# Convolution, attention and mixture of experts on one core: the last part in a fixed periodic order, transposes moved to VectorE, roots moved to ScalarE

## The chip, the core and the metric

The kernel runs on one core of a Trainium2 chip. The core has five engines that run side by side, each of them in the order in which its instructions were written: TensorE (PE in the profile; its weight loads are listed as PEld), VectorE (DVE), ScalarE (ACT), GpSimd (POOL) and SyncE (SP), which here only issues DMAs. An instruction waits on semaphores until what it needs is there, and everything behind it on its engine waits with it. The metric is the device time of one launch in microseconds; the median of several runs counts.

## The reference

Thirty-two images of 128 channels and 64 x 64 pixels go through three steps. Cut to what matters:

```python
# layer 0: butterfly transforms along h and w, one mix over channels per frequency, and back
x = x + conv(gn(x))                       # complex; real part is taken
# layer 1: 4096 tokens of 128 channels per image
t = tokens(x)
n = ln(t)                                 # mean and variance of each token, eps 1e-5
k, v = n @ Wk.T + bk, n @ Wv.T + bv
probs = softmax(einsum('sbe,sbf->sef', k, v) / sqrt(seq_len))
t = t + einsum('sef,sbf->sbe', probs, n)
n = ln(t)
p = softmax(n @ router_w + router_b)      # 8 experts, the best 2 with renewed weights
t = t + sum over the best 2 of p * (n @ expert_w[e] + expert_b[e])
x = channels(t)                           # back to (128, 64, 64)
```

For the attention, `seq_len` is the size of the first axis, 32, and each image has its own 128 x 128 table of scores. All arithmetic is in 32-bit floats.

## The kernel before

The kernel has three parts. The first transforms every image, the second mixes channels per frequency; the last products of the mixing start at 2527.08 us. The third part, which the change is about, takes everything after that: inverse transform, attention, experts, and the way back to channels. It handles image after image, and three images are in work at once: while image b is in its inverse transform (`conv`), b-1 is in its attention (`front`), and b-2 in its experts (`experts`).

**Names of the steps.** Each step is added to a planner under a short key; the profile shows tile names and lines.

- `r0..r7` (SP, L887) load the mixed frequencies of an image from DRAM, `x` (SP, L879) loads the image itself. `w0..w7` (PE, tile pu, L903) transform along w, `wo` (ACT, tile u, L913) copies out, `h0..h3` (PE, tile py, L925) transform along h, `ho` (DVE, L933) adds to the image tile y.
- `pt0..pt7` (PE, L1049) turn 512 pixels each from channels to tokens, four 128 x 128 transposes; `to` (ACT, L1054) copies into the token buffer tk (two buffers, one for even, one for odd images); `sa` (DVE, L1021) takes statistics. `va` (DVE, six small operations on 128 x 32 values, L1031 to L1036) makes variances of them, `pwa` (POOL, L1041) takes the power -0.5, `na` (DVE, L1078 and L1079) makes the shift.
- `xg` (ACT, L1089) normalizes, `pg` (PE, L1100) makes the Gram matrix, then a short chain of small steps (`gs`, `pb`, `t1`, `pb2`, `sm`, `pr`, `sr`, `sn`, `pc`, `prx`) makes the softmax. `pp` (PE, L1173) applies it to the image tile (the image is the stationary operand), `at` (ACT, L1186) scales, `ad` (DVE, L1201) adds to tk.
- `vb`, `pwb`, `nb` do the same as `va`, `pwa`, `na` for the second norm (`nb`: L1240 and L1241). `lg`, `l2`, `f1` to `f5`, `gt` (DVE, L1232 to L1276) make logits, find the best two experts and their gates.
- `xn` (ACT, L1301) normalizes, `px` (PE, L1311) transposes, `xT` (ACT, L1317) copies, `pe` (PE, L1324) multiplies 128 tokens by four experts, `m` (DVE, L1335) weighs the result out of PSUM, `s` (POOL, L1360 to L1363, five operations) sums over experts into tk.
- `st` (PE, tile po, L1370) transposes 512 tokens back to channels, and `so` (ACT, L1376) copies them to SBUF and issues one DMA of 256 KB to the output (L1377).

**What sets the order.** The planner (`Plan.run`) is a list scheduler that runs when the program is built: each step has an engine, an estimated cost, a due time (with offsets in `SHIFT`), the steps it follows, and the buffers it takes and frees. Buffers matter below: `pe` has three PSUM banks, shared by the expert products, so the fourth product waits until `m` has read the first; `tl` has three banks for all of `pt`, `px`, `st`, `pg`, `pp` and the softmax chain; `cv` is one tile for `w` and `h`.

Of the kernel before, what the change touches and what calls it, by code (L numbers as in the profile page):

```python
# [24 lines left out]
class Plan:  # L25
# [12 lines left out]
    def run(self):  # L38
# [46 lines left out]
        self.length = now  # L85
        for i in order:
            ops[i][3]()
# [3 lines left out]
def kernel(  # L91
# [737 lines left out]
    def prepare():  # L829
# [23 lines left out]
    plan = Plan({"cv": 1, "pe": 3, "tl": 3, "r": 10, "x": 2, "xg": NG, "xn": 2, "xT": 2, "tm": 2, "so": 2, "gate": 2})  # L853
    SLOT = 114.0

    SHIFT = {
        "ad": -0.15, "at": -0.25, "f": 0.71, "gs": -1.97, "gt": 0.71, "h": -0.24, "ho": -3.5, "kvp": 3.43,
        "kvq": -0.45, "l": 0.71, "lg": 3.61, "m": -0.32, "na": -1.87, "nb": -0.81, "pb": -1.97, "pc": -1.97,
        "pe": 0.16, "pg": -0.08, "pp": 0.19, "pr": -1.97, "prx": -1.97, "pt": -0.23, "pwa": -1.87, "pwb": 3.61,
        "px": 0.15, "r": -0.04, "s": 0.08, "sa": 1.29, "sm": -1.97, "sn": -1.97, "so": 2.13, "sr": -1.97,  # L860
        "st": 1.1, "t": -1.97, "to": 0.06, "va": -1.87, "vb": 3.61, "w": 0.28, "x": -0.68, "xT": -0.68,
        "xg": 0.21, "xn": 2.42,
    }
    made = {}

    def add(b, key, engine, us, at, run, after=(), take=(), free=(), late=0.0):


        names = [k if isinstance(k, tuple) else (b, k) for k in after]
        at += SHIFT.get(key.rstrip("0123456789_"), 0.0)  # L870
        made[b, key] = plan.add(
            engine, us, SLOT * at, run, [made[k] for k in names if k[0] >= 0], take, free, late
        )


    def transfers(b):
        def load_x():
            xs[b] = xp.tile([P, HW, HW], F32, tag="x", name=f"y{b}")
            nc.sync.dma_start(xs[b].rearrange("c h w -> c (h w)"), xv[b])  # L879

        def load_r(e):
            def run():
                i = 8 * b + e
                ring, tag = (rp, "r") if i % 10 < 8 else (rp2, "r2")
                t = rs[b, e] = ring.tile([P, 16 * n], F32, tag=tag, name=f"r{b}_{e}")
                for r in range(2):
                    nc.sync.dma_start(t[r * n : (r + 1) * n], pfv[b, e, r])  # L887
            return run

        for e in range(8):  # L890
            add(
                b, f"r{e}", "SP", 0.2, b - 0.5 + 0.08 * e, load_r(e) if b else (lambda: None), take=("r",),
                late=5.0 if b else 0.0,
            )
        add(b, "x", "SP", 0.1, b + 0.2, load_x if b else (lambda: None), take=("x",), late=12.0 if b else 0.0)

    def conv(b):
        def w_inverse(e):

            def run():  # L900
                ps = tile_of["cv", b, e] = cps.tile([P, 8, P], F32, tag="cv", name=f"pu{b}_{e}")
                for k in range(8):
                    nc.tensor.matmul(  # L903
                        ps[:, k, :], rs[b, e][:, k * P : (k + 1) * P], qw.rearrange("w r m -> w (r m)"),
                        start=True, stop=True,
                    )
            return run
# [31 lines left out]
        def w_inverse_piece(e, oh):  # L939

            def run():
                ps = tile_of["cw", b, e, oh] = eps.tile([P, 8, n], F32, tag="pe", name=f"pw{b}_{e}_{oh}")
                for k in range(8):
                    lo = (2 * k + oh) * n
                    for r in range(2):
                        nc.tensor.matmul(
                            ps[r * n : (r + 1) * n, k, :], rs[b, e][:, lo : lo + n], qw[:, r, :], start=True, stop=True
                        )
            return run
# [28 lines left out]
        if b < 2:  # L978
            for e in range(8):
                at = b + 0.08 * e  # L980
                for oh in range(2):
                    add(
                        b, f"w{e}_{oh}", "PE", 0.95, at + 0.04 * oh, w_inverse_piece(e, oh),
                        [f"r{e}"] + [(b - 1, f"h{k}") for k in range(4)], ("pe",), ("r",) if oh else (),
# [13 lines left out]
            if b == 0:  # L998
                add(b, "prep", "PE", 3.5, 0.98, prepare, ["h3"], ("pe",), ("pe",))
# [14 lines left out]
    def front(b):  # L1014
# [24 lines left out]
        def power(which):  # L1039
            total, var, nmr, rstd = v[which]  # L1040
            nc.gpsimd.tensor_tensor(rstd, var, mhalf, ALU.pow)  # L1041

        def turn(g):
            def run():
                ps = tile_of["pt", b, g] = tps.tile([P, 512], F32, tag="tl", name=f"pt{b}_{g}")
                x1 = xs[b].rearrange("c h w -> c (h w)")
                for k in range(4):
                    i = 4 * g + k
                    nc.tensor.transpose(ps[:, k * P : (k + 1) * P], x1[:, i * P : (i + 1) * P], ident)  # L1049
# [18 lines left out]
        for g in range(8):  # L1068
            at = s1 + 0.016 * g
            add(b, f"pt{g}", "PE", 0.48, at, turn(g), [(b - 2, f"st{g}")] + [f"ho{k}" for k in range(4)], ("tl",))  # L1070
            add(b, f"to{g}", "ACT", 0.55, at, turned(g), [f"pt{g}"], (), ("tl",))
            add(b, f"sa{g}", "DVE", 0.85, at, stats1(g), [f"to{g}"] + (["sa0"] if g else []))
        add(b, "va", "DVE", 1.7, s1 + 0.14, lambda: moments(1), [f"sa{g}" for g in range(8)])
        add(b, "pwa", "POOL", 5.5, s1 + 0.14, lambda: power(1), ["va"])

        def nmr1():
            total, var, nmr, rstd = v[1]
# [3 lines left out]
        add(b, "na", "DVE", 0.9, s1 + 0.14, nmr1, ["pwa"])  # L1081
# [74 lines left out]
        add(b, "pb", "PE", 0.35, at, kv1, ["gs"], ("tl",))  # L1156
# [10 lines left out]
        def product(lo, m):  # L1167
            def run():
                x1 = xs[b].rearrange("c h w -> c (h w)")
                ps = tile_of["pp", b, lo] = tps.tile([P, 512], F32, tag="tl", name=f"pp{b}_{lo}")  # L1170
                for k in range(m):
                    i = lo + k
                    nc.tensor.matmul(  # L1173
                        ps[:, k * QX : (k + 1) * QX], x1[:, i * P : (i + 1) * P], prx[b % 2], start=True, stop=True
# [30 lines left out]
        for j, lo in enumerate(range(0, NT, 3)):  # L1205
            m = min(3, NT - lo)
            at = s1 + 0.45 + 0.016 * j
            add(b, f"pp{lo}", "PE", 0.26 * m, at, product(lo, m), ["prx", (b - 1, "lg")], ("tl",), ("x",) if lo == 30 else ())
# [29 lines left out]
        def nmr2():  # L1238
            total, var, nmr, rstd = v[2]
# [41 lines left out]
        add(b, "pwb", "POOL", 5.5, at, lambda: power(2), ["vb"])  # L1281
        add(b, "lg", "DVE", 1.95, at, logits1, ["vb"])
        add(b, "nb", "DVE", 2.1, at + 0.1, nmr2, ["pwb", "lg"])
        add(b, "l2", "DVE", 1.95, at + 0.1, logits2, ["nb"], ("gate",))
# [7 lines left out]
    def experts(b):  # L1292
# [73 lines left out]
        def back(g):  # L1366
            def run():
                ps = tile_of["po", b, g] = tps.tile([P, 512], F32, tag="tl", name=f"po{b}_{g}")
                for k in range(4):
                    nc.tensor.transpose(ps[:, k * P : (k + 1) * P], t[:, 4 * g + k, :], ident)  # L1370
            return run

        def store(g):
            def run():
                so = wp.tile([P, 512], F32, tag="so", name=f"so{b}_{g}")
                nc.scalar.copy(so, tile_of.pop(("po", b, g)))  # L1376
                nc.sync.dma_start(ov[b][:, g * 512 : (g + 1) * 512], so)  # L1377
# [3 lines left out]
        for g in range(8):  # L1381
            at = s2 + 0.125 * g
            add(b, f"xn{g}", "ACT", 1.65, at - 0.1, normal(g), ["nb"], ("xn",))
            add(b, f"px{g}", "PE", 0.48, at - 0.05, turn(g), [f"xn{g}"], ("tl", "xT"), ("xn",))
            add(b, f"xT{g}", "ACT", 0.55, at - 0.05, turned(g), [f"px{g}"], (), ("tl",))
            for k in range(4):
                i = 4 * g + k
                for half in range(2):
                    add(
                        b, f"pe{i}_{half}", "PE", 0.86, at + 0.125 * (2 * k + half) / 8, expert(i, half), [f"xT{g}"],  # L1390
                        ("pe",), ("xT",) if k == 3 and half else (),
# [6 lines left out]
                        ("pe",) + (("gate",) if i == NT - 1 and half else ()),  # L1398
# [8 lines left out]
            add(b, f"st{g}", "PE", 0.48, at + 0.25, back(g), [f"s{2 * g}", f"s{2 * g + 1}"], ("tl",))  # L1407
            add(b, f"so{g}", "ACT", 0.55, at + 0.25, store(g), [f"st{g}"], (), ("tl",))
# [6 lines left out]
    plan.run()  # L1415
# [53 lines left out]
```

## Time and profile before

| | |
|---|---|
| median of three runs | 6039.6 us (6039.03 to 6046.36) |
| profiled execution, its own time | 6034.45 us |
| span of that profile | 6032.7 us |
| busy over the span: PE, PEld, DVE, ACT, POOL | 98%, 77%, 70%, 62%, 70% |
| third part, steady stretch of 27 images | 2852.74 to 5724.84 us |
| PE busy in it | 2835.63 of 2872.10 us |
| stretch from the end of the mixing to 2852.74 us | 325.74 us, PE busy 296.94 |
| stretch from 5724.84 us to the end | 308.16 us, PE busy 272.10 |

The page of a profile gives busy time for each engine; groups of instructions are listed as `line engine op out<-in shape xcount | busy us, mean ns | idle before it <- releaser`. A matmul in 32-bit floats shows as two instructions (two passes), a transpose as one. PE matmuls overlap in the records, so that the time which one group takes is read from the distance between its start and the start of the next group, not from its mean.

### The profile page before, as it was taken

To read this page: it belongs to the slowest core of one execution; us is meant where nothing else is said; L and a number is where in the kernel's file an instruction comes from. 1 tells how busy PE (TensorE), PEld (TensorE's weight loads), DVE (VectorE), ACT (ScalarE), POOL (GpSimd) and SP (SyncE) were. 2 spreads that over 40 slices of the span, in tenths; PEclk is the share of its full clock that TensorE was granted. 3 is DMA by queue.
4 is the path that set the end of the run, shared out by engine and by line. 5 is a ranking of instruction groups with operands and counts; after the bars stand their busy time and mean duration, and the time that the engine had idled before them with its cause. 6 is when DMAs were issued, how large, how long until landed. Compare 5 with 4: busy or idle time off the path is not lost.

```text
span 6032.7 us, 219314 instructions
## 1 busy us (share of the span) xinstructions
PE 5884.8 (98%) x95372; PEld 4672.1 (77%) x95372; DVE 4220.6 (70%) x7696; ACT 3757.1 (62%) x7057; POOL 4205.9 (70%) x3793
## 2 busy tenths in 40 slices
PE   7999999999999999989999999999999999999998
PEld 7999999999999999866666666666666666666654
DVE  5565545555555555458778787887878788787888
ACT  7666664555555555467766676676767666676663
POOL 2110006666666666538898998989899888998988
PEclk9999999999999999999999999999999999999999
DMA  5767766666666666632222122221322222132100
GB/s 198 240 226 236 236 217 192 174 172 173 171 173 173 171 173 172 171 102 88 81 71 98 57 98 71 83 86 57 106 63 91 78 74 95 57 100 70 66 27 28
DMA packets 554068, 756.74 MB, mean 125 GB/s; under 512 B 58320, under 2 KB 318928, under 8 KB 549008
## 3 DMA queue, kind: packets, MB, share of 16 engines
q1 hardware_dynamic: 550496, 733.64, 40.3%
q8 instruction: 749, 12.27, 0.9%
q0 software_dynamic: 2608, 9.06, 0.5%
q14 instruction: 215, 1.76, 0.1%
HBM read 406.79 MB, written 335.54 MB: 123 GB/s over the span
## 4 chain that ended last, share of the span: by engine, by line
PE 88%; ACT 7%; issue 2%; DVE 1%; POOL 1%; DMA 1%; SPq 0%; POOLq 0%; ACTq 0%; DVEq 0%
PE pe L1324 28%; PE m L658 17%; PE g L636 9%; PE pf L418 7%; PE pu L903 6%; PE pp L1173 4%; PE py L925 4%; PE pg L1100 4%; PE pv L396 3%; PE px L1311 2%; ACT xn L1301 2%; ACT u L913 2%; PE pz L373 1%; ACT z L383 1%; PE pt L1049 1%
## 5 line engine op out<-in xcount | busy, mean ns | idle before, releaser
L1324 PE MATMUL pe<-ew_sb,xT 128*128 128x512 f32 x4096 | 1946.1, 597 | 19.4 <-DVE tm L1335 16.0
L1335 DVE TENSOR_TENSOR tm<-pe,oh 128x512 f32<-128x512 f32 x2028 | 1346.4, 684 | 479.3 <-PE pe L1324 455.5
L1360 POOL TENSOR_TENSOR tm<-tm 128x512 f32<-128x512 f32 x1014 | 1286.1, 1284 | 201.1 <-DVE tm L1335 182.7
L1324 PEld LDWEIGHTS pe<-ew_sb,xT 128*128 128x128 f32 x4096 | 700.9, 191 | 522.9 <-issue 396.1
L647 DVE COPY f<-g 128x1024 f32<-128x1024 f32 x508 | 622.2, 1225 | 648.9 <-PE g L636 648.9
L658 PE MATMUL m<-f,s 128*64 128x64 f32 x32768 | 1070.1, 224 | 1.9 <-issue 1.1
L658 PEld LDWEIGHTS m<-f,s 128*64 128x64 f32 x32768 | 1000.0, 138 | 63.2 <-issue 2.6
L604 POOL COPY s<-l 128x512 f32<-128x512 f32 x512 | 546.0, 1099 | 524.9 <-issue 508.3
L647 ACT COPY f<-g 128x1024 f32<-128x1024 f32 x508 | 514.5, 1013 | 561.0 <-PE g L636 534.8
L1363 POOL TENSOR_TENSOR tk<-tk,tm 128x256 f32<-128x256 f32 x1014 | 753.6, 743 | 79.5
L1361 POOL TENSOR_TENSOR tm<-tm 128x512 f32<-128x512 f32 x507 | 650.4, 1283 | 39.8
L913 ACT COPY u<-pu 64x512 f32<-64x512 f32 x960 | 556.6, 580 | 135.1 <-PE pu L903 121.5
L636 PE MATMUL g<-c,wst 9*128 9x128 f32 x16256 | 599.9, 283 | 3.6 <-issue 3.3
L636 PEld LDWEIGHTS g<-c,wst 9*128 9x128 f32 x16256 | 502.8, 186 | 38.5 <-issue 3.9
L349 POOL TENSOR_TENSOR grstd<-gms,mhalf 128x1 f32<-128x1 f32 x32 | 17.8, 555 | 735.8 <-DVE gms L345 735.8
L1186 ACT ACTIVATE pp<-pp,m 128x128 f32<-128x128 f32 x1024 | 440.9, 431 | 124.1 <-PE pp L1173 99.3
L606 POOL TENSOR_SCALAR s<-l 128x512 f32<-128x512 f32 x256 | 509.5, 1990 | 0.0
L903 PEld LDWEIGHTS pu<-qw,r 128*128 128x128 f32 x3840 | 455.7, 193 | 63.3 <-ACT u L913 49.5
L903 PE MATMUL pu<-qw,r 128*128 128x128 f32 x3840 | 476.3, 278 | 25.6 <-ACT u L913 25.6
L1317 ACT COPY xT<-px 128x512 f32<-128x512 f32 x256 | 150.2, 587 | 560.5 <-PE px L1311 557.5
L418 PE MATMUL pf<-ph,v 128*128 128x128 f32 x4096 | 491.0, 278 | 5.0 <-ACT z L383 1.1
L418 PEld LDWEIGHTS pf<-ph,v 128*128 128x128 f32 x4096 | 466.9, 192 | 14.7 <-ACT z L383 7.1
(177 smaller groups left out, 8573.0 us busy)
## 6 DMA issues: line engine op xcount, KB each, us to landing
xf<-f SPq DMA_DIRECT2D x512, 256.0 KB
pf<-o SPq DMA_DIRECT2D x1016, 128.0 KB
l<-xf SPq DMA_DIRECT2D x1012, 128.0 KB
r<-pf SPq DMA_DIRECT2D x496, 256.0 KB
x<-in_x_dram SPq DMA_DIRECT2D x256, 256.0 KB
out_dram<-so SPq DMA_DIRECT2D x256, 256.0 KB
y<-in_x_dram SPq DMA_DIRECT2D x31, 2048.0 KB
r<-pf POOLq DMA_DIRECT2D x16, 248.0 KB, 7.7
```

Source lines behind the costliest of these rows:

```text
L418: nc.tensor.matmul(pl[:, j * P : (j + 1) * P], vs[b][:, 8 * g + j, :], ph.rearrange("h r m -> h (r m)"), start=True, stop=True,)
L604: nc.gpsimd.tensor_copy(dst, src)
L636: nc.tensor.matmul(pg[g // 2][:, g % 2, m * P : (m + 1) * P], wst[rows, 16 * half + 4 * t + m, :], c[rows].rearrange("r h k -> r (h k)"), ...
L647: copy(f.rearrange("i m (g o) -> i m g o", g=2), tile_of["g", w, half, t][k].rearrange("i g (o m) -> i m g o", o=4))
L658: nc.tensor.matmul(ps[hh * n : (hh + 1) * n, q, :], s[:, h].rearrange("i k b -> i (k b)")[:, B * r : B * r + n], f[:, h, r, :], start=(r = ...
L903: nc.tensor.matmul(ps[:, k, :], rs[b, e][:, k * P : (k + 1) * P], qw.rearrange("w r m -> w (r m)"), start=True, stop=True,)
L913: nc.scalar.copy(u[r * n : (r + 1) * n, :, oh * n + 8 * e : oh * n + 8 * e + 8], ps[oh * n : (oh + 1) * n, :, r * n : (r + 1) * n].rearran ...
L1324: nc.tensor.matmul(ps, tile_of["xT", b, i // 4][:, i % 4, :], ew_sb[:, es, :].rearrange("d e c -> d (e c)"), start=True, stop=True,)
L1335: nc.vector.tensor_tensor(tile_of["tm", b, i // 2][:, i % 2, es, :], tile_of.pop(("pe", b, i, half)).rearrange("p (e c) -> p e c", c=P), t ...
L1360: nc.gpsimd.tensor_tensor(tm[:, k, 0:4, :], tm[:, k, 0:4, :], tm[:, k, 4:8, :], ALU.add)
L1361: nc.gpsimd.tensor_tensor(tm[:, :, 0:2, :], tm[:, :, 0:2, :], tm[:, :, 2:4, :], ALU.add)
L1363: nc.gpsimd.tensor_tensor(t[:, lo : lo + 2, :], t[:, lo : lo + 2, :], tm[:, :, m, :], ALU.add)
```

## The change

The change leaves the first two parts alone and alters four things in the third.

1. The tokens of a group of 512 are dealt out differently: token tile i of the group holds pixels 4p + i instead of 128 i + p. So `pt` and `pp` read the image tile with a step of four values (16 bytes) between neighbours.
2. The way back to channels (`st` on PE and the copy of `so` on ACT) is replaced by one VectorE instruction for 512 tokens (`flip`, key `so`), which transposes blocks of 32 x 32 and writes with a step of four values. The store (`os`, on SP) is four DMAs of 32 partitions each, in pieces of 512 bytes, instead of one DMA in pieces of 2 KB.
3. The power -0.5 on POOL becomes `Ln` and `Exp` on ACT, followed by one Newton step on DVE, three small operations at the head of `na` and `nb`.
4. The planner's order is replaced by a written one: `ORDER` lists the steps of one period with an image offset, `EDGE` shifts them for the first two and the last two images, and `follow` issues them so. Waits for `x`, `xT` and gate buffers are written as dependencies, the loads take whichever ring buffer came free, and `prep` runs after the first statistics.

```diff
+    def follow(self, order):
...
-    plan = Plan({"cv": 1, "pe": 3, "tl": 3, "r": 10, "x": 2, "xg": NG, "xn": 2, "xT": 2, "tm": 2, "so": 2, "gate": 2})
+    plan = Plan({"cv": 1, "pe": 3, "tl": 3, "r": 10, "xg": NG, "xn": 2, "tm": 2, "so": 2})
...
         def power(which):
             total, var, nmr, rstd = v[which]
-            nc.gpsimd.tensor_tensor(rstd, var, mhalf, ALU.pow)
+            nc.scalar.activation(rstd, var, AF.Ln)
+            nc.scalar.activation(rstd, rstd, AF.Exp, scale=-0.5)
+
+        def newton(which):
+            total, var, nmr, rstd = v[which]
+            nc.vector.scalar_tensor_tensor(var, var, -0.5, rstd, ALU.mult, ALU.mult)
+            nc.vector.tensor_tensor(var, var, rstd, ALU.mult)
+            nc.vector.scalar_tensor_tensor(rstd, var, 1.5, rstd, ALU.add, ALU.mult)
...
-                x1 = xs[b].rearrange("c h w -> c (h w)")
+                x1 = xs[b].rearrange("c (g h) w -> c g (h w)", g=8).rearrange("c g (p i) -> c g i p", i=4)
                 for k in range(4):
                     i = 4 * g + k
-                    nc.tensor.transpose(ps[:, k * P : (k + 1) * P], x1[:, i * P : (i + 1) * P], ident)
+                    nc.tensor.transpose(ps[:, k * P : (k + 1) * P], x1[:, i // 4, i % 4, :], ident)
...
-                        ps[:, k * QX : (k + 1) * QX], x1[:, i * P : (i + 1) * P], prx[b % 2], start=True, stop=True
+                        ps[:, k * QX : (k + 1) * QX], x1[:, i // 4, i % 4, :], prx[b % 2], start=True, stop=True
...
-        def back(g):
-            def run():
-                ps = tile_of["po", b, g] = tps.tile([P, 512], F32, tag="tl", name=f"po{b}_{g}")
-                for k in range(4):
-                    nc.tensor.transpose(ps[:, k * P : (k + 1) * P], t[:, 4 * g + k, :], ident)
+        def flip(g):
+            def run():
+                so = tile_of["so", b, g] = wp.tile([P, 4, 32, 4], F32, tag="so", name=f"so{b}_{g}")
+                nc.vector.transpose(
+                    out=so.rearrange("p k w t -> p t k w"),
+                    in_=t[:, 4 * g : 4 * g + 4, :].rearrange("p t (k c) -> p t k c", c=32),
+                )
...
-                so = wp.tile([P, 512], F32, tag="so", name=f"so{b}_{g}")
-                nc.scalar.copy(so, tile_of.pop(("po", b, g)))
-                nc.sync.dma_start(ov[b][:, g * 512 : (g + 1) * 512], so)
+                so = tile_of.pop(("so", b, g)).rearrange("p k w t -> p k (w t)")
+                for a in range(4):
+                    nc.sync.dma_start(
+                        ov[b][:, g * 512 + a * P : g * 512 + (a + 1) * P].rearrange("(k c) m -> c k m", c=32),
+                        so[32 * a : 32 * a + 32],
+                    )
...
+    ORDER = """
+        s2:4 na:3 m8_1:4 xg0:3 h3:2 m9_0:4 xg2:3 xg1:3 pe9_1:4 pe10_0:4 m9_1:4 pe11_0:4 s4:4 so0:4 m10_0:4 xg3:3
...
+        m20_1:4 w2:1 xT6:4 ad12:3 s10:4 vb:3 pe24_0:4 wo2_0:1 pe25_1:4 m24_0:4 wo2_1:1 px7:4 m25_1:4 x:1 pe24_1:4
+        pwb:3 lg:3 pe25_0:4 w3:1 m25_0:4 m24_1:4 s12:4 nb:3 pe26_0:4 wo3_0:1 pe26_1:4 m26_0:4 wo3_1:1 m26_1:4 pt4:2
+        xn0:3 l2:3 pe27_0:4 pt3:2 pe27_1:4 m27_0:4 to4:2 w4:1 xT7:4 m27_1:4 f1:3 s13:4 px0:3 wo4_0:1 r7:0 r2:0
...
+        px4:3 pe5_1:3 pe5_0:3 va:2 pe4_1:3 m5_1:3 pwa:2 h2:1 m4_1:3 m5_0:3 pe8_0:3 ho2:1 xT3:3 pe8_1:3 m8_0:3
+        pe9_0:3
+    """
+    EDGE = {
...
+    plan.follow(list(dict.fromkeys(i for at, i in sorted(turns))))
```

## The prediction

> **What bounds the kernel now.** I read the page first, then one period of the third part in four views: busy time by stretch, groups by line, the timeline, the chain of waits. On the page PE is busy for 98% of the span; the first two parts are not touched, so the question is what the third costs per image. The chain shows the same PE pieces every 106.37 us (2852.74, 2959.12, 3065.49), so one image costs one such period. Busy time by stretch, one period (span, then PE, PEld, DVE, ACT, POOL, clock, DMA share, GB/s):
>
> ```profile
> 2959.12:3065.49 106.37, 105.02 (x744) 71.81 (x744) 85.44 (x190) 73.01 (x168) 95.20 (x83) 1.00 0.24 80
> ```
>
> PE has 1.35 us of visible idle; POOL is next with 95.2, then DVE with 85.4. The groups of the steady stretch (27 images) name what idles PE, and the groups to be removed:
>
> ```profile
> L903 PE MATMUL pu<-qw,r 128*128 128x128 f32 x3456 | 423.8, 276 | 14.4 <-ACT u L913 14.4
> L1049 PE MATMUL pt<-ident,y 128*128 128x128 f32 x865 | 131.4, 274 | 21.4 <-ACT tk L1054 21.4
> L1370 PE MATMUL po<-ident,tk 128*128 128x128 f32 x864 | 130.4, 273 | 0.6
> L1376 ACT COPY so<-po 128x512 f32<-128x512 f32 x216 | 121.6, 592 | 82.8 <-PE po L1370 82.2
> L1041 POOL TENSOR_TENSOR m<-m,mhalf 128x32 f32<-128x32 f32 x55 | 299.2, 5440 | 39.5 <-DVE m L1036 39.5
> L1078 DVE SCALAR_TENSOR_TENSOR m<-m 128x32 f32<-128x32 f32 x27 | 17.9, 664 | 0.0
> L1240 DVE SCALAR_TENSOR_TENSOR m<-m 128x32 f32<-128x32 f32 x27 | 26.9, 995 | 0.0
> L1036 DVE SCALAR_TENSOR_TENSOR m<-m 128x32 f32<-128x32 f32 x54 | 10.4, 192 | 1.9
> ```
>
> See the last three: the same small operation takes 192, 664 or 995 ns. What a PE group really takes is the distance between starts in the timeline:
>
> ```profile
> 4022.69 5.32 PE L1324 MATMUL pe<-ew_sb,xT 128*128 128x512 f32 x12
> 4027.84 0.60 PE L1370 MATMUL po<-ident,tk 128*128 128x128 f32 x4
> 4028.28 1.95 PE L903 MATMUL pu<-qw,r 128*128 128x128 f32 x16
> 4030.07 0.60 PE L1049 MATMUL pt<-ident,y 128*128 128x128 f32 x4
> ```
>
> Twelve `pe` passes take 5.15 us, four transposes 0.436 (not 0.60), sixteen `pu` passes 1.79. In the same way a `py` group takes 2.02, `pg` 0.89, `pp` 0.735. Per image: pe 128 x 0.429 = 54.9; pu 8 x 1.79 = 14.3; pt, px and po 24 x 0.436 = 10.5; py 4 x 2.02 = 8.1; pg 8 x 0.89 = 7.1; pp 10 x 0.735 + 0.49 = 7.8; the softmax chain 0.7. Sum 103.4. The period has 3.0 more: 35.8 / 27 = 1.3 named waits (pt, pu), and 1.7 of small losses where the operation changes.
>
> Last, DVE and POOL in the tail, where POOL works without a break (timeline):
>
> ```profile
> 5827.08 1.30 DVE L1032 TENSOR_TENSOR m<-bs 128x32 f32<-128x32 f32 x1
> 5828.31 1.30 DVE L1033 TENSOR_TENSOR m<-bs 128x32 f32<-128x32 f32 x1
> 5829.53 0.18 DVE L1034 TENSOR_TENSOR m<-m 128x32 f32<-128x32 f32 x1
> ...
> 5827.05 2.49 POOL L1360 TENSOR_TENSOR tm<-tm 128x512 f32<-128x512 f32 x2
> ```
>
> Each of two 0.2 us operations ends as one of POOL's 1.25 us instructions ends: it is held until then.
>
> **What the Trainium skill says.** "SBUF — State Buffer", section "Who interferes with whom": a DVE instruction with two SBUF inputs contends with a GpSimd instruction that reads SBUF, and the later one blocks fully. The lines above agree (1.30 against 0.2). The same page (section on the DMA port swizzle) speaks of 16-byte lines, with a penalty when each access crosses to a new one, and calls four 32-bit values the limit of free striding. The new reads step by exactly that; no row of before has such a PE read. "ScalarE: Activation LUTs", section "What ACT_TABLE_LOAD costs": 1283 ns for the load and about 2.66 us with a drain; the only one before took 1283. "VectorE: DVE Perf Modes", section "The three transpose paths": VectorE transposes blocks of 32 x 32 only, 311 ns for 128 x 128 in bf16; no transpose of DVE is in the trace.
>
> **The change, part by part.**
>
> *Transposes off PE.* 8 x 0.436 = 3.49 us of PE per image go, and 8 of the takes of the `tl` banks with them. PE's sum becomes 99.9. ACT loses 8 x 0.59 = 4.7.
>
> *Flips on DVE.* Eight instructions of 128 x 512. Near rows: L1335 with as many values takes 0.68 and follows itself every 0.60. I take 0.61, so 4.9 per image. Bounds: 0.55 (one value a cycle without overhead, from L933, 1024 values in 1.225) and 1.15 (two passes); the upper one adds 4.3 to DVE, of which I let 2.6 reach PE, because flips stand between the `m` that free PE's banks.
>
> *Strided reads on PE.* 32 passes of `pt` and 64 of `pp` read their stationary operand with the step. Now a pass of `pt` takes 0.109 us and one of `pp` 0.1225 with loads hidden. Bounds: nothing, and a doubled load, 32 x 0.107 + 64 x (0.214 - 0.1225) = 9.3 us per image. I take nothing: DVE and ACT copy with far larger PSUM steps at full rate (L913: 512 values in 0.58), and a 32-bit load is slow enough, one column in about 0.84 ns.
>
> *Roots.* POOL loses 2 x 5.44 = 10.9 per image. The instruction list of the changed kernel has a table load before each `Ln` and each `Exp`, 128 in all, so ACT gains 4 x 1.28 + 4 x 0.23 (as L1267) = 6.05, in two blocks of 3.05. Bounds: 3.05 and, with the drain, 5.8. I take 3.05; nothing in the row says that the engine stays shut. ACT ends at 73.0 - 4.7 + 6.05 = 74.3. Behind each block wait `wo` copies and `xT`. The three new DVE operations of a root depend on each other and read two SBUF inputs: 0.2 each if free (0.6), 1.3 each if held (3.9). I take 0.4 each, 1.2. DVE then has 85.4 + 4.9 + 2.4 = 92.7.
>
> *The order.* I laid the two tight stretches out with these steps. Second root: from the end of `w2`, PE does seven `pe` products, px7, pt4, pt3 and w3 before it needs the bank that m26_0 frees for pe27_1: 7 x 0.86 + 3 x 0.436 + 1.79 = 9.1. Meanwhile ACT copies wo2 (0.2 + 2.4), takes the root (3.05 + 0.13), then `nb` (2.55: 1.35 of today plus 1.2), then m26_0 (0.77): 9.1. The margin is nil. First root: from the start of `va` the other side takes 1.27 + 3.18 + 0.2 (m8_0 in front) + 2.05 (`na`) + 0.77 (m8_1) = 7.47; PE reaches pe10_0 after 0.24 + 2 x 2.02 + 4 x 0.86 = 7.72. The margin is 0.26. Everything that makes these roots longer goes straight to PE, because m26_0 and m8_1 are queued behind `nb` and `na`. Elsewhere pe29_0 waits about 0.3 for m28_0 behind `f1`. The waits of pt and pu go: `tl` has fewer takers, and w3 and w4 lie five products apart. I put new waits at 0.9: that 0.3 and 0.6 for held operations in `nb`.
>
> *Stores and loads.* SP issues 32 store DMAs per image instead of 8, at 0.34 to 0.45 each 11 to 14 us; it now stands idle for 61.55 us at a stretch (4055.38). Pieces of 512 bytes: the second part loads such rows and moves 190 GB/s (200 to 2500 us), so 2 MB are about 11 us of a period whose DMA share is 0.24. Cost nothing; if the cover fails, a late `r` stops `w` on PE. `prep` moves by some 30 us within image 0's start; the same work, nothing.
>
> Sum: 99.9 + 1.7 + 0.9 = 102.5 per image, 3.87 less than now. Over 31 periods 120 us. The two ends hold 28.8 + 36.1 us of idle PE; they are only shifted, so 0, give or take 20. From the profiled 6034.45 that is 5914; the median of the runs is 5.2 above it: 5920.
>
> **The rivals.** (1) *POOL holds DVE at the roots, slower than before.* POOL no longer stands in its power at that time but sums, and `na` and `nb` have five small operations each, ten per image. For: the tail rows (1.30), L1078 and L1240 (664 and 995 with a 0.2 us base). Against: POOL is free for 15% of the period, and operations slip in between its instructions (L1034). If all six new ones are held, 2 x (3.9 - 1.2) = 5.4; if today's four are held too (0.9 for `na`'s and 1.0 for `nb`'s over today), 7.3; less the 0.26 and the 0.6 already counted, 6.4 on 102.5 = 108.9. It decides from 3.9 on: four more held operations. Time about 5920 + 31 x 5.2 = 6080. (2) *Half of it*: one or two operations held per root, or flips of 1.15 us: 2.6 per image, about 6000. For: DVE at 92.7 of 102.5 in strict order. (3) *Tables with drain*: 2 x 2.75 - 0.26 = 5.2 less the 0.6, so 4.6: about 6060, near no change. Against: the row of 1283. (4) *Strided loads doubled*: 9.3, about 6200. (5) *No new waits and shorter ends*: 101.6 and 20 us, about 5870.
>
> **How the numbers follow.** Forecast (5870 to 5965) 0.56; half of it (5965 to 6035) 0.19; held roots 0.11; drain 0.05; strided loads 0.05; better 0.04. The likeliest gives 5920. The range 5865 to 6045 holds the first two, most of the drain and a part of the better case, 0.79. 0.2% (12 us) is about what a measurement can tell from no change. Faster: 0.56 + 0.19 + 0.04 = 0.79; the drain case is split, 0.03 to "same" and 0.02 to "slower", and 0.01 of the held roots goes to "same": same 0.04, slower 0.17.
>
> **What would show it.** The period as repeated in the chain: 102.5, and no PE idle before pt and pu. Transposes of 0.6 us on DVE; `pt` groups still 0.436 and `pp` 0.735 apart; table loads of 1.28 with the next activation right behind. New idle before `pe` released by DVE at pe27_1 and pe10_0 gives the rivals their size, together with the durations of the Newton operations. It would be wrong if these exceed 0.4 us on average by much, or if `pt` spreads out.

## The result and the profile after

The changed kernel takes 6249.43 us (median of four runs, 6242.68 to 6259.01) against 6039.45 us (four runs, 6039.03 to 6046.36). The ratio is 1.0346, 95% interval 1.0328 to 1.0364. It is 210 us slower; the forecast was 120 us faster. The profiled execution took 6242.68 us, its span is 6240.9.

The chain of waits of the changed kernel still repeats, now every 112.32 us where the granted clock stays at 1.00. Busy time by stretch for one period (span, then PE, PEld, DVE, ACT, POOL, clock, DMA share, GB/s):

```profile
3804.54:3916.86 112.32, 108.69 (x711) 76.01 (x711) 99.03 (x204) 74.78 (x168) 84.67 (x80) 1.00 0.28 76
```

One image costs 5.95 us more than the 106.37 of before, although PE has 33 instructions fewer. Times 31 that is 184 us of the profiled difference of 208. Of the other 24, drops of the clock (below) take about 6, and 1.4 had arisen before the third part (the last products of the mixing start at 2528.52 instead of 2527.08); the rest lies at the two ends, which were not taken apart. VectorE gained 13.6 us and POOL lost 10.5. The groups of the steady stretch (3000 to 5800 us, 24.9 images) show where PE's time went; the columns are busy time, mean ns of one, idle time before:

```profile
L1342 PE MATMUL pe<-ew_sb,xT 128*128 128x512 f32 x3184 | 1555.9, 601 | 94.1 <-DVE tm L1353 94.1
L907 PE MATMUL pu<-qw,r 128*128 128x128 f32 x3152 | 388.3, 277 | 0.0
L1190 PE MATMUL pp<-prx,y 128*128 128x144 f32 x1600 | 387.3, 377 | 0.0
L1063 PE MATMUL pt<-ident,y 128*128 128x128 f32 x792 | 121.6, 281 | 0.0
```

The waits of `pt` and `pu` are gone. In their place PE stands 94.1 us before `pe`, 3.77 per image, released by VectorE. And a pass of `pp` has a mean of 377 ns, against 288 in the kernel before. The weight loads of the two steps that read the image (the same view, engine PEld):

```profile
L1190 PEld LDWEIGHTS pp<-prx,y 128*128 128x128 f32 x1600 | 415.0, 322 | 98.9 <-issue 41.8 <-DVE prx L1169 6.5 <-PE pp L1190 6.0
L1063 PEld LDWEIGHTS pt<-ident,y 128*128 128x128 f32 x792 | 122.1, 204 | 81.5 <-issue 68.9 <-ACT tk L1068 6.2 <-ACT u L918 6.0
```

Before, these loads took 190 and 141 ns (groups of the kernel before, PEld, 2740 to 6033 us):

```profile
L1173 PEld LDWEIGHTS pp<-prx,y 128*128 128x128 f32 x1920 | 270.7, 190 | 116.3 <-issue 92.8 <-PE pp L1173 20.8 <-DVE tm L1335 0.5
L1049 PEld LDWEIGHTS pt<-ident,y 128*128 128x128 f32 x960 | 110.9, 141 | 46.6 <-ACT tk L1054 29.9 <-issue 16.3
```

What that does to PE is seen in the distance between starts (timelines of PE; first a `pp` group of the kernel before, then the changed kernel):

```profile
4093.44 0.90 PE L1173 MATMUL pp<-prx,y 128*128 128x144 f32 x6
4094.17 1.02 PE L1324 MATMUL pe<-ew_sb,xT 128*128 128x512 f32 x2
```

```profile
3926.26 0.63 PE L1063 MATMUL pt<-ident,y 128*128 128x128 f32 x4
3926.73 2.11 PE L1342 MATMUL pe<-ew_sb,xT 128*128 128x512 f32 x4
...
3968.26 1.45 PE L1190 MATMUL pp<-prx,y 128*128 128x144 f32 x6
3969.54 1.02 PE L1342 MATMUL pe<-ew_sb,xT 128*128 128x512 f32 x2
```

A `pp` group of three takes 1.287 us (six passes of 0.21) instead of 0.735, one of two 0.82 instead of 0.49: ten and one per image, 5.85 us. A `pt` group takes 0.472 instead of 0.436: 0.29 us per image. The two reads have the same step. The load of `pt` grew by 63 ns and stays nearly hidden, that of `pp` by 132 (means; the median at a step of four is 329) and does not; why the same step costs the transpose's load less, no run here tells.

On VectorE and ScalarE (groups of the same stretch) see the flip, the Newton step, the operation behind it, and the table loads:

```profile
L1387 DVE STREAM_TRANSPOSE so<-tk 128x512 f32<-128x512 f32 x200 | 223.4, 1117 | 0.6
L1054 DVE TENSOR_TENSOR m<-m 128x32 f32<-128x32 f32 x49 | 52.1, 1063 | 1.7
L1259 DVE TENSOR_SCALAR m<-m 128x32 f32<-128x32 f32 x24 | 23.2, 968 | 0.8
L1055 DVE SCALAR_TENSOR_TENSOR m<-m 128x32 f32<-128x32 f32 x49 | 43.1, 880 | 1.7
L1053 DVE SCALAR_TENSOR_TENSOR m<-m 128x32 f32<-128x32 f32 x49 | 14.1, 288 | 0.0
...
L1047 ACT ACT_TABLE_LOAD x50 | 64.2, 1283 | 0.9
L1048 ACT ACTIVATE m<-m 128x32 f32<-128x32 f32 x49 | 11.3, 230 | 0.5
```

A Newton step costs 0.288 + 1.063 + 0.880 = 2.23 us. Why, the timeline at the second root shows, with both engines side by side:

```profile
3889.45 0.18 DVE L1053 SCALAR_TENSOR_TENSOR m<-m 128x32 f32<-128x32 f32 x1
3889.61 2.50 POOL L1378 TENSOR_TENSOR tm<-tm 128x512 f32<-128x512 f32 x2 [3.42 <-DVE tm L1353]
3889.66 1.26 DVE L1054 TENSOR_TENSOR m<-m 128x32 f32<-128x32 f32 x1
...
3890.96 1.20 DVE L1055 SCALAR_TENSOR_TENSOR m<-m 128x32 f32<-128x32 f32 x1
...
3892.18 1.32 POOL L1379 TENSOR_TENSOR tm<-tm 128x512 f32<-128x512 f32 x1
...
3892.41 1.13 DVE L1259 TENSOR_SCALAR m<-m 128x32 f32<-128x32 f32 x1
3893.45 1.28 DVE L1353 TENSOR_TENSOR tm<-pe,oh 128x512 f32<-128x512 f32 x2
...
3894.19 1.13 PE L1342 MATMUL pe<-ew_sb,xT 128*128 128x512 f32 x2 [1.67 <-DVE tm L1353]
```

The first Newton operation slips in ahead of POOL and takes 0.18. The second ends at 3890.92, where the first of POOL's two sums is over, the third at 3892.16, where the second is. Behind them stands m26_0, and behind that pe27_1, which PE starts 1.67 us late. The prediction named this place.

A late `pe` has a second price. In some images (timeline of PE, then busy time by stretch; the seventh figure, behind POOL's, is the granted clock):

```profile
4006.52 1.36 PE L1342 MATMUL pe<-ew_sb,xT 128*128 128x512 f32 x2 [1.84 <-DVE tm L1353]
...
4007.67 3.40 PE L907 MATMUL pu<-qw,r 128*128 128x128 f32 x16
```

```profile
4007.67:4010.90 3.23, 3.23 (x17) 3.23 (x16) 3.19 (x5) 0.98 (x2) 1.67 (x2) 0.53 0.00 0
3895.15:3896.93 1.78, 1.78 (x17) 1.78 (x16) 1.75 (x3) 1.15 (x3) 1.37 (x1) 1.00 0.00 0
```

The same sixteen `pu` passes take 3.23 us at a granted clock of 0.53 after PE stood for 1.84 us, and 1.78 at full clock in an image where it stood for 1.67. The length of the wait alone does not decide it: between 2960 and 5760 us PE stood for 1.84 us five times, and three of these waits were followed by a drop (4006.52, 4119, 4682), two not (2992, 5357).

### The profile page after: what moved, and what is told of

It reads as the page before. It is cut to its first block, busy times and chain, and to the rows that moved or that the text cites. A ratio compares the mean times of both kernels' runs of the same rounds, so it can differ in the third digit from the quotient of the medians.

```text
span 6240.9 us, 218089 instructions
## 1 busy us (share of the span) xinstructions
PE 6002.9 (96%) x94348; PEld 4810.3 (77%) x94348; DVE 4653.3 (75%) x8144; ACT 3812.5 (61%) x7057; POOL 3865.2 (62%) x3729
## 3 DMA queue, kind: packets, MB, share of 16 engines
q14 instruction: 224, 1.84, 0.1%
## 4 chain that ended last, share of the span: by engine, by line
PE 74%; DVE 19%; issue 3%; ACT 3%; DMA 1%; POOL 1%; DVEq 0%; SPq 0%; ACTq 0%; POOLq 0%
PE pe L1342 19%; PE m L671 17%; PE g L649 9%; PE pp L1190 7%; PE pf L431 6%; DVE tm L1353 6%; PE pu L907 4%; PE pg L1117 4%; PE pv L409 3%; DVE bs L1027 2%; PE py L930 2%; PE pz L386 1%; ACT z L396 1%; PE pt L1063 1%; DVE m L1054 1%
## 5 line engine op out<-in xcount | busy, mean ns | idle before, releaser
L1342 PE MATMUL pe<-ew_sb,xT 128*128 128x512 f32 x4096 | 2004.0, 603 | 150.2 <-DVE tm L1353 142.7
L1353 DVE TENSOR_TENSOR tm<-pe,oh 128x512 f32<-128x512 f32 x2028 | 1325.7, 684 | 272.3 <-PE pe L1342 242.4
L1342 PEld LDWEIGHTS pe<-ew_sb,xT 128*128 128x128 f32 x4096 | 687.6, 192 | 655.9 <-DVE tm L1353 315.4
L1190 PEld LDWEIGHTS pp<-prx,y 128*128 128x128 f32 x2048 | 529.9, 323 | 124.4 <-issue 51.2
L907 PEld LDWEIGHTS pu<-qw,r 128*128 128x128 f32 x3840 | 468.8, 195 | 79.8 <-issue 54.4
L1190 PE MATMUL pp<-prx,y 128*128 128x144 f32 x2048 | 496.5, 378 | 1.6 <-DVE tk L1218 0.8
L1106 ACT ACTIVATE xg<-tk,m 128x128 f32<-128x128 f32 x1024 | 397.9, 482 | 139.0 <-DVE m L1096 137.1
```

The costliest lines, as they stand in the source:

```text
L907: nc.tensor.matmul(ps[:, k, :], rs[b, e][:, k * P : (k + 1) * P], qw.rearrange("w r m -> w (r m)"), start=True, stop=True,)
L1190: nc.tensor.matmul(ps[:, k * QX : (k + 1) * QX], x1[:, i // 4, i % 4, :], prx[b % 2], start=True, stop=True)
L1342: nc.tensor.matmul(ps, tile_of["xT", b, i // 4][:, i % 4, :], ew_sb[:, es, :].rearrange("d e c -> d (e c)"), start=True, stop=True,)
L1353: nc.vector.tensor_tensor(tile_of["tm", b, i // 2][:, i % 2, es, :], tile_of.pop(("pe", b, i, half)).rearrange("p (e c) -> p e c", c=P), t ...
```

## The experiments

The kernel before was timed beside each group of runs; its medians were 6044.87 (e1 to e4), 6050.55 (e5 to e8), 6045.94 (e9 to e11) and 6040.41 (e12, e13). Ratios are to these, with 95% intervals. The new order by itself, with roots, way back and token order as before, was not run; e8 and e9 each put one old part back into it.

| run | what differs | median us | ratio |
|---|---|---|---|
| e1 | after, pp without step | 6103.12 | 1.0093 (1.0078 to 1.0108) |
| e2 | after, no Newton step | 6163.08 | 1.0193 (1.0178 to 1.0208) |
| e3 | e1 and e2 together | 6019.45 | 0.9953 (0.9936 to 0.9970) |
| e4 | before, pp with step of four | 6239.95 | 1.0320 (1.0305 to 1.0336) |
| e5 | after, flip writes without step | 6228.08 | 1.0292 (1.0276 to 1.0307) |
| e6 | after, consecutive tokens, no Newton | 5995.35 | 0.9908 (0.9893 to 0.9923) |
| e7 | before, roots on ScalarE | 6131.51 | 1.0135 (1.0118 to 1.0152) |
| e8 | e6 with the way back on PE | 6172.50 | 1.0203 (1.0188 to 1.0218) |
| e9 | e6 with the roots on POOL | 6126.12 | 1.0130 (1.0113 to 1.0147) |
| e10 | after, step of two, no Newton | 5982.74 | 0.9891 (0.9876 to 0.9905) |
| e11 | e6 with the Newton step | 6071.13 | 1.0040 (1.0025 to 1.0055) |
| e12 | e10, additions of 1 on ScalarE | 5970.36 | 0.9884 (0.9868 to 0.9901) |
| e13 | before, pp with step of eight | 6242.07 | 1.0334 (1.0313 to 1.0354) |

**e1, pp without the step.** Theory: the strided weight load, on PE's own path. Rival: VectorE paces the period.

```diff
-                        ps[:, k * QX : (k + 1) * QX], x1[:, i // 4, i % 4, :], prx[b % 2], start=True, stop=True
+                        ps[:, k * QX : (k + 1) * QX], x1[:, i * P : (i + 1) * P], prx[b % 2], start=True, stop=True
```

> Edit: only the product with the image (pp) reads 128 consecutive pixels as its stationary operand again; pt keeps the step of four, so products are added to other tokens than they belong to. Theory A (the strided stationary operand costs PE 0.55 us per pp group of three, 5.9 us per image, and PE sets the period): 31 x 5.9 = 183 us less, about 6066; pp groups of three 0.735 us apart again. Rival B (DVE paces the period at the roots, so PE only waits longer there): more than 6190, and the idle time before pe grows from 3.6 to over 7 us per image.

6103.12, 146 us less than the changed kernel. Groups of e1 (PE, 3000 to 5700 us, 25.1 images):

```profile
L1342 PE MATMUL pe<-ew_sb,xT 128*128 128x512 f32 x3208 | 1571.3, 603 | 105.0 <-DVE tm L1353 102.9 <-DMA r<-pf 1.9
L907 PE MATMUL pu<-qw,r 128*128 128x128 f32 x3216 | 406.5, 281 | 0.0
L1190 PE MATMUL pp<-prx,y 128*128 128x144 f32 x1600 | 241.0, 286 | 0.0
```

`pp` is back at its old pass. The missing 37 us have two places: the wait before `pe` grows from 3.77 to 4.18 per image, 13 us over 31 (at pe25_0, behind `vb`, alone from 0.92 to 1.90); and drops of the clock get frequent. Summed over stretches of 4 us from 2960 to 5760, they lose 18.6 us in e1 and 5.1 in the changed kernel, so some 16 more over the third part. That is 29 of the 37. Theory A holds with this correction, B is out.

**e2 and e3, no Newton step.** The root is left as log and exp give it.

```diff
         def nmr1():
-            newton(1)
...
         def nmr2():
-            newton(2)
```

> Edit: the Newton step of both roots is left out (three VectorE operations each); the root is what log and exp give. Theory A (the held Newton operations, 2.2 us per root, are most of the new wait of PE before pe): PE idle before pe falls from 3.7 to about 0.5 us per image, 31 x 3.2 = 100 us less, about 6150. Rival B (the wait comes from the flips and the gate operations, which stay): within 35 us of the changed kernel, 6215 or more.

6163.08, 86 us less. The same view of e2:

```profile
L1340 PE MATMUL pe<-ew_sb,xT 128*128 128x512 f32 x3154 | 1532.7, 600 | 36.8 <-DVE tm L1351 36.8
```

The wait falls to 1.5 us per image, not 0.5: the 1.67 us at pe27_1, behind the second Newton step, are gone, and what is left is chiefly 0.92 us at pe25_0. In the steady stretch no drop of the clock was found. Removing 4.46 us of VectorE per image was worth 2.8 of the period: theory A, somewhat smaller.

> Edit: both of the edits before together (pp on consecutive pixels, no Newton step). Theory A (two separate costs, both on PE's path): they add up, 6249 - 183 - 100 = about 5966, period about 103. Rival B (DVE, with the flips of 1.12 us, becomes the bound as soon as PE is faster): 6060 or more, with PE idle before pe of 3 us or more per image.

6019.45: 230 us less than the changed kernel, where 146 + 86 = 232 would be the plain sum. The two costs are separate, but each is smaller than was taken, so the sum is 53 us above the 5966 expected: PE still waits 2.2 us per image before `pe`, 1.90 of it at pe25_0, and some of these waits are followed by drops of the clock. Both edits together are just enough to make the change a gain.

**e4 and e13, the step alone in the kernel before.**

```diff
-                x1 = xs[b].rearrange("c h w -> c (h w)")
+                x1 = xs[b].rearrange("c (g h) w -> c g (h w)", g=8).rearrange("c g (p i) -> c g i p", i=4)
...
```

> Edit to the kernel before: its pp reads every fourth pixel of 512 as stationary operand, nothing else; products are added to other tokens than they belong to. Theory A: 5.9 us per image on PE also in the old order, 31 x 5.9 = 183 us more, about 6222, a ratio of 1.030. Rival (the 3 us per period that the old order loses to waits take part of it): 6150 or less, ratio below 1.018.

6239.95, 195 us more, with its period at 112.58 us (4123.11 to 4235.69). This one access pattern costs nearly what the whole change does. Not even the old order's idle time hides it.

> Edit to the kernel before: pp alone reads its stationary operand with a step of eight values out of 1024 pixels (products are added to other tokens than they belong to). At two the load took 196 ns, at one 190, at four 329 (6240 us in this kernel). Theory A (every value out of another piece of 16 bytes costs the same, however far apart): load about 330 ns and about 6240 us as at four. Theory B (the price grows with the span that is read): load over 500 ns and more than 6600 us.

6242.07, the same as at four within the intervals. Groups of e13, engine PEld:

```profile
L1173 PEld LDWEIGHTS pp<-prx,y 128*128 128x128 f32 x1536 | 398.8, 329 | 69.9 <-issue 28.7 <-PE pp L1173 17.2
```

So the price does not go by the span that is read: theory A.

**e5, the flip without the step.**

```diff
-                    out=so.rearrange("p k w t -> p t k w"),
+                    out=so.rearrange("p k w t -> p (k w t)").rearrange("p (t k w) -> p t k w", t=4, k=4),
```

> Edit to the changed kernel: the flip writes its output tile in consecutive order (values of the output therefore land at other pixels), everything else as it is. Theory A (1.12 us is what transposing 128 x 512 values of 32 bits takes, whatever the step of the output): flips still 1.1 us, time within 25 us of 6249. Theory B (the 16-byte step of the output doubles it): flips about 0.6 us, VectorE 4.1 us less per image, of which 1 to 2 reach PE, about 6200.

```profile
L1387 DVE STREAM_TRANSPOSE so<-tk 128x512 f32<-128x512 f32 x193 | 135.2, 701 | 0.6
```

The flip (groups of e5, DVE) falls from 1.117 to 0.701 us: theory B's mechanism, the step of the output. The time, 6228.08, is 21 us less; allowing for the slightly slower kernel before that was timed beside it the gain is 33. That is 0.7 to 1.1 us of the 3.3 that VectorE saves per image, at the low end of what was expected. A flip is mostly off the path.

**e6, tokens of consecutive pixels.** No operand of PE has a step, the flip writes runs of 32 values, stores go out in pieces of 128 bytes. No Newton step. The part on the flip and the store:

```diff
-                    out=so.rearrange("p k w t -> p t k w"),
+                    out=so,
...
-                    nc.sync.dma_start(
...
+                    for tt in range(4):
+                        lo = g * 512 + tt * P + 32 * a
+                        nc.sync.dma_start(
+                            ov[b][:, lo : lo + 32].rearrange("(k c) m -> c k m", c=32), so[32 * a : 32 * a + 32, tt]
+                        )
```

> Edit to the changed kernel: tokens are 128 consecutive pixels again everywhere (pt and pp read without a step), the flip writes consecutive runs of 32 values and the store sends them in pieces of 128 bytes with 128 DMAs per image; no Newton step. Theory: as with both edits before (6019), 0.3 us per image less for pt, about 6010; if the flip also gets cheaper (theory B of the flip) 5960 to 5990. Rival (small store pieces hold up SP or the loads of r): 6060 or more, with waits of PE or ACT for DMA.

5995.35, faster than both kernels, and just above the 5960 to 5990 expected with a cheaper flip. PE waits 50.0 us in 26 images before `pe`, 1.9 each (1.2 of it at pe25_0), and no wait of PE or ACT names a DMA. 128 store DMAs per image are hidden.

**e7, the roots alone in the kernel before.** Same order, same place, no Newton step.

```diff
-            nc.gpsimd.tensor_tensor(rstd, var, mhalf, ALU.pow)
+            nc.scalar.activation(rstd, var, AF.Ln)
+            nc.scalar.activation(rstd, rstd, AF.Exp, scale=-0.5)
```

> Edit to the kernel before: its two roots per image by log and exp on ScalarE, without a Newton step, in the old order and at the same place; nothing else. Theory A (the roots alone are free; POOL's 10.9 us were not on PE's path, and ACT has room for two blocks of 3.05 us): 6044 within 20 us. Rival (the blocks make xT or the copies of u late in the old order): 1 to 3 us per image more, 6075 to 6140, with new PE waits for ACT.

6131.51, 81 us more, in the rival's range but by another mechanism: PE waits for VectorE (40.8 us in 25 images), not for ACT. The timeline of e7 behind `vb` shows `lg`, whose four operations ran in 0.42 us each in the kernel before:

```profile
3529.95 2.50 POOL L1361 TENSOR_TENSOR tm<-tm 128x512 f32<-128x512 f32 x2 [1.20 <-DVE tm L1336]
...
3531.19 1.53 DVE L1234 TENSOR_TENSOR lg<-lq,m 128x256 f32<-128x256 f32 x1
...
3532.52 1.33 POOL L1362 TENSOR_TENSOR tm<-tm 128x512 f32<-128x512 f32 x1
...
3532.76 1.37 DVE L1235 TENSOR_TENSOR lg<-lg,lq 128x256 f32<-128x256 f32 x1
...
3536.52 1.12 PE L1325 MATMUL pe<-ew_sb,xT 128*128 128x512 f32 x2 [1.47 <-DVE tm L1336]
```

In the kernel before POOL was in its power at this point (3062.38 to 3067.82, beside `lg` at 3064.11 to 3065.78):

```profile
3062.38 5.44 POOL L1041 TENSOR_TENSOR m<-m,mhalf 128x32 f32<-128x32 f32 x1 [0.60 <-DVE m L1036]
3064.11 0.42 DVE L1233 TENSOR_TENSOR lg<-lq,m 128x256 f32<-128x256 f32 x1
```

The power does not hold VectorE, and while it ran POOL could not start the sums, which do. Taking the power away uncovered `lg`. The waits behind it are 1.65 us per image, 51 us over 31, and drops of the clock take some 14 more; the other 16 of the 81 are not accounted for.

**e8 and e9, parts of e6 taken back.** e8 transposes back on PE with a copy on ScalarE, placed where a `tl` bank is free in the new order (the steps that depend on it move along):

```diff
-                nc.vector.transpose(
...
+                for k in range(4):
+                    nc.tensor.transpose(ps[:, k * P : (k + 1) * P], t[:, 4 * g + k, :], ident)
+                nc.scalar.copy(so, ps)
```

> Edit to the changed kernel: tokens consecutive, no Newton step, and the way back by PE transposes with a copy on ScalarE as in the kernel before, put into the new order where a tl bank is free. Differs from the run with consecutive tokens only in the way back. Theory A (the flips take 3.5 us off PE and give most of it back as waits for VectorE): within 25 us of that run, PE idle before pe under 1 us per image. Rival (the flips keep their 3.5 us): 80 us or more above that run.

6172.50, 177 us above e6: theory A was wrong. The transposes themselves are 31 x 3.49 = 108 us. The rest is new waits, chiefly for `tl` banks (waits of PE in e8):

```profile
PE pt L1063 <- ACT so L1388: 16.9, 25, 0.7
PE pg L1116 <- ACT so L1388: 16.9, 25, 0.7
PE pb L1133 <- ACT so L1388: 16.2, 24, 0.7
```

These are 2.0 us per image. Waits before `pu` and the transposes add 0.8, and the wait before `pe` falls from 1.9 only to 1.2: together 64 of the other 69 us. So in this order the flips are worth having. How much of the new waits belongs to the places I chose for the transposes stays open.

e9 puts POOL's power back into e6 (the diff of e7 the other way round).

> Edit to the kernel with consecutive tokens and no Newton step (5995): its roots are POOL's power again, no log and exp on ScalarE; order unchanged. Theory A (in this order the root's length counts, its neighbours are free of POOL anyway): 5.44 instead of 3.05 us, up to 2.4 us more at each root, of which PE feels 2 to 5 us per image, 6060 to 6150. Theory B (POOL's power keeps POOL's sums away from VectorE, and that cover is worth more than the root's length): the held small operations fall to 0.2 to 0.4 us and PE's idle before pe falls below 1.9 us per image, 5950 to 5990.

6126.12, 131 us above e6: theory A. PE waits 127.7 us in 25 images, 5.1 each, 98 us more over 31; drops of the clock lose 25.5 us in the steady stretch against 1.6 in e6. VectorE now stands 2.1 us at the second root, and 2.0 at the first, until the power is done (groups of e9):

```profile
L1255 DVE SCALAR_TENSOR_TENSOR m<-m 128x32 f32<-128x32 f32 x25 | 31.2, 1248 | 52.4 <-POOL m L1047 52.4
```

But the neighbours are not free of POOL, as theory A had it: POOL goes from its power straight into sums, and this operation is held to 1.25 us (0.18 in e6). So the root's length and the held operations behind it both count here; the run does not part them. So, without a Newton step, the roots on ScalarE cost 81 us in the old order and save 131 in the new one.

**e10, a step of two.** Tokens are dealt out of 256 pixels; two flips of half the size, pieces of 256 bytes. No Newton step.

```diff
-                x1 = xs[b].rearrange("c (g h) w -> c g (h w)", g=8).rearrange("c g (p i) -> c g i p", i=4)
+                x1 = xs[b].rearrange("c h w -> c (h w)").rearrange("c (g p i) -> c g i p", p=P, i=2)
```

> Edit to the changed kernel: tokens are dealt out of 256 pixels with a step of two (8 bytes) instead of 512 with four, for pt, pp, the flip (two instructions of 128 x 256) and the store (pieces of 256 bytes); no Newton step. Against the kernel with consecutive tokens (5995). Theory A (the weight load pays in proportion to the span it reads, half of the price at four): pp groups of three about 0.87 us apart instead of 0.735 (1.29 at four), 30 to 60 us more. Theory B (any step other than one doubles it): 1.29 us apart, about 180 us more. Theory C (a step of 8 bytes is free): 0.735, within 30 us.

5982.74; its ratio overlaps that of e6. Groups of e10:

```profile
L1189 PE MATMUL pp<-prx,y 128*128 128x144 f32 x1664 | 250.6, 286 | 0.0
```

```profile
L1189 PEld LDWEIGHTS pp<-prx,y 128*128 128x128 f32 x1664 | 245.8, 196 | 135.1 <-issue 103.5 <-DVE bs L1027 12.4 <-DVE prx L1168 6.8
```

Theory C for `pp`: at two the load takes 196 ns and the pass is that of no step. The load of `pt` is another matter (same view):

```profile
L1063 PEld LDWEIGHTS pt<-ident,y 128*128 128x128 f32 x835 | 127.7, 202 | 86.0 <-issue 74.0 <-ACT u L918 6.0 <-ACT tk L1068 6.0
```

It takes 202 ns at a step of two, as good as the 204 at four, against 141 without a step; hidden as it is, it costs PE little (a group takes 0.46 to 0.47 us).

**e11, e6 with the Newton step.**

> Edit to the changed kernel: consecutive tokens for pt, pp, flip and store as before, the Newton step kept. Theory (the costs add up as they did with the step of four): 86 us above the 5995 without Newton plus a few us for drops of the granted clock, 6080 to 6100, so still slower than the kernel before. Rival (the cheaper flips of 0.70 us give VectorE room for the Newton operations): below 6040.

6071.13, 76 us above e6 and, by its interval, slower than the kernel before. With its roots refined as the change has them, the new order loses even when every read is consecutive.

**e12, the additions of 1 on ScalarE.**

```diff
-            nc.vector.tensor_scalar_add(nmr, nmr, 1.0)
...
+                if g == 0:
+                    nc.scalar.activation(nmr, nmr, AF.Copy, bias=1.0)
```

> Edit to the kernel with a step of two and no Newton step (5983): the last operation of each root on VectorE, the addition of 1 that takes 1.04 and 1.25 us there while POOL works, is done by ScalarE just before its first use of the result; the same arithmetic. Theory (small VectorE operations held by POOL right behind a root are what PE still waits for): VectorE 2.3 us less per image at the two places, PE's idle before pe falls from 1.73 to 0.6 to 1.0 us per image, 20 to 35 us less, 5945 to 5965. Rival (the next operation behind is held in its place, as POOL works on): within 10 us of 5983.

5970.36, the fastest median, but its ratio cannot be told from that of e10. PE still waits 44.9 us before `pe`, against 46.3 in e10, though two operations of 1.04 and 1.25 us are gone from VectorE. The number is the rival's, and part of its mechanism is seen: `lg` (L1269), the next operation with two SBUF inputs behind the second root, grows from 409 ns in e10 to 1020. But the theory had also named the wrong place. Most of what PE still waits for lies ahead of the second root, at pe25_0 (timeline of PE in e12):

```profile
4098.80 1.12 PE L1342 MATMUL pe<-ew_sb,xT 128*128 128x512 f32 x2 [1.32 <-DVE tm L1353]
```

In e10 that wait is 1.33 of 1.78 us per image, and it stands behind two held operations of `vb`, of 1.3 us each, which neither run touched.

## Why the prediction was wrong

*Strided reads: the step that failed.* The term put at "nothing" was worth 6.1 us per image, 190 us over 31. The bound was there: a doubled load, 9.3, of which 5.86 for `pp` (measured 5.85) and 3.4 for `pt` (measured 0.29). Its 0.107 us for a load is an estimate, what 128 columns take at the rate of a `pe` pass (512 in 0.429 us); the records of the loads are longer, 190 and 141 ns. The case against a cost rested on ScalarE's and VectorE's reads of PSUM, which say nothing of a weight load from SBUF. The Trainium skill ("SBUF — State Buffer", section on the DMA port swizzle) asks for two hits in each 16-byte line and then calls four 32-bit values free. The loads of `pp` agree with the first and not with the second: 190, 196, 322 and 329 ns (means) at steps of one, two, four and eight. With a step of four each 16 bytes hold one value that is read. The load of `pt` fits neither: it pays the same at two (202) as at four (204). That lines of 16 bytes are the cause is the page's account; the runs show only where the price begins. I read the second sentence and gave the case a chance of 0.05.

*Roots: a term mis-sized.* 1.2 us per Newton step; it took 2.23. Its mechanism was in the rivals, with its price. e2 puts it at 86 us. The table loads took 1.28 with the activation right behind, as taken. Not foreseen was what e7 shows: POOL's power was a cover. The new order keeps `lg` clear of the sums (0.42 each). Of the 13.6 us that VectorE gained, the flips are 8.9 and the Newton steps 4.5, so its other operations together took no longer than before. Single ones did: the six of `va` or `vb` sum to 2.91 us instead of 1.79 (means).

*Waits of the new order.* Forecast 0.9, measured 3.77. The margins were right about the place: nil at pe27_1, which waits 1.67 to 1.84. pe29_0 waits 0.72 (forecast 0.3). pe1_1 waits 0.33. pe25_0, 0.92 behind the held operations of `vb`, was missing (timelines of VectorE and PE):

```profile
3882.01 1.30 DVE L1038 TENSOR_TENSOR m<-bs 128x32 f32<-128x32 f32 x1
3883.36 1.27 DVE L1040 TENSOR_TENSOR m<-m 128x32 f32<-128x32 f32 x1
3886.09 1.13 PE L1342 MATMUL pe<-ew_sb,xT 128*128 128x512 f32 x2 [0.92 <-DVE tm L1353]
```

pe10_0, with a margin of 0.26, shows no wait.

*Flips.* 0.61 taken, 1.117 measured, close to the upper bound of 1.15; without the step 0.70 (e5). I let 2.6 of 4.3 reach PE; e5 gives 0.7 to 1.1 of 3.3.

*What held.* Transposes off PE: 3.49 gone, and of e8's 177 us they are 108. The waits before `pt` and `pu` went. Stores cost nothing, even with 128 DMAs per image (e6; in e10 one wait of PE, 1.3 us, names a store).

The sum: 102.5 forecast, + 6.1 for the reads, + 2.9 for the waits, gives 111.5. The last 0.8 sits in small losses that no view names; the drops of the clock, 0.2 per image on average, come on top, as the period of 112.32 has none. That rival (4) at 6200 lies near the measured time is in part luck: it took 9.3 for the reads, which cost 6.1, and nothing more for the waits, which cost 2.9. Two figures of the working do not hold: the drain case at 6060 lies outside the range up to 6045 that was to hold most of it, and POOL, with 84.3 of 102.5 us, would have been free for 18%, not 15%.

## What to carry to other kernels

Price an access pattern per engine and operand. A step that costs one reader little can make another's load 1.7 times as long (190 to 322 ns), and if that is on the engine that bounds the kernel, every image pays it. Before taking work off an engine that is not the bound, ask what it kept from running: what it starts instead may hold the engine that matters. In an order without slack, the small operations between the last arrival and the next product decide, so price them as held; and before taking one away, look whether a wait stands behind it (e12).

## What the runs showed of the hardware that was not expected

- The weight load of `pp`: 6 ns more at a step of 8 bytes, 132 more at 16, 139 more at 32. That of `pt`: 61 more at 8, 63 more at 16. The 128 x 512 transpose on VectorE pays for a 16-byte step of its output too: 1117 against 701 ns.
- The granted clock can fall to about half for some 3.3 us after PE has stood, which costs about 1.5 us each time. It followed some waits of 1.8 to 2.3 us and not others (in e3 a wait of 2.06 us at 4028.27 had none), and in e7 some of 1.48 that were followed by one of 0.34 after 1.1 us of work. None of the 27 waits of 1.33 in e10 was followed by a drop, and none was found in the steady stretch of the kernel before or of e2, whose longest waits were 0.8 and 0.9 us. The Trainium skill ("TensorE: Matmul & The Clock Gate", section "What's actually happening") gives half the clock after an idle window of about 3.4 us; here shorter waits were enough in some images, and what decides between the images stays open.
- POOL's power on 128 x 32 values (5.44 us) lets VectorE's operations with two SBUF inputs run beside it in 0.42 us (128 x 256), the time that they also take in the new order clear of POOL's sums; beside the sums they took 0.83 to 1.53 in e7. So the rule that the prediction quotes held for the sums and not for the power, which reads SBUF too.
